# A fifth of the score products, and two residual sums, made on GpSimd in a four-layer graph network

## The chip, the cores and the metric

One NeuronCore of a Trainium2 chip runs the whole kernel. The metric is device time in microseconds. Every run in this study was in the fast state, so all comparisons are of like with like. Engine names are those of the profile: PE (matmuls), PEld (weight loads), DVE (VectorE), ACT (ScalarE), POOL (GpSimd), SP (issues DMAs).

## The reference, cut to what matters

16 graphs of 1024 nodes with 128 features go through four graph layers. The costly one is layer 2, done twice per graph: each edge gets a score from a small network, the scores weigh the adjacency, and messages are summed.

```python
# layer 2, for each of two rounds l (B = 16, N = 1024, D = 128); adjacency has some 1.6% nonzeros
a = x @ We1[l, :D];  b = x @ We1[l, D:]
h = relu(a[:, :, None, :] + b[:, None, :, :] + be1[l])
scores = sigmoid(h @ We2[l] + be2[l])
messages = (adjacency * scores) @ x
... # update by a two-layer network, residual, layer norm
# around every layer: x = x + layer(relu(layernorm(x)))
```

## The kernel before, where the change touches it

The kernel computes scores only for existing edges. Edges of a 128x128 block sit in slots (320, or 480 on the diagonal). One-hot matrices `on`, `om` (fp8), and their transposes `onT`, `omT`, gather node terms to slots and scatter scores back, all by matmuls. A round has nine groups of four blocks: seven off-diagonal (two directions d, so eight products) and two diagonal (four products).

Per group: PE makes `pre`; ACT and DVE make `hid` from it; PE makes `sc`; ACT makes the scores; then this runs:

```python
def scores(self):
    ...
    pt = path.bank("sc", f"pt_{name}")            # scores, slots now on partitions (PSUM)
    ...                                           # u: the scores as two f16 halves (SBUF)
    for d in range(self.nd):
        for i in range(Q):                        # Q = 4
            if i % 2 == 0:
                pair = ...path.m.scratch(...)      # one buffer holds two products
            j = i * self.nd + d
            right = (self.s.omT if d else self.s.onT)[self.grp[i]]
            v = u[:, :, j % J, j // J : j // J + 1]
            nc.vector.tensor_tensor(              # val: the product of one-hot and score
                pair[:, i % 2, :ck], right[:, :ck], v.to_broadcast([P, ck, P]), op=OP.mult
            )
            self.val[d, i] = pair[:, i % 2]

def scatter(self, part):                          # PE; part 0..3, spread over the next group
    ...
    nc.tensor.matmul(self.ps[d][:, i], left[:, k], halves[:, k, :, h], ...)   # reads val
```

Both inputs of a product lie in SBUF: the one-hots and the scores. The residual sums are `nc.vector.tensor_add(xt, xt, o)` at the end of layer 1, and `nc.vector.tensor_add(xt, xt, new)` after layer 2. Each is followed by a layer norm whose statistics DVE makes and whose -0.5 power POOL makes (the only work of POOL).

A scheduler orders every engine's instructions at build time. In the trace of the kernel before, DVE and POOL run theirs in the order built (13 of DVE's 10,759 records could not be matched), so an instruction that waits holds up those behind it.

## Time and profile before

| | before |
|---|---|
| time, median (lowest to highest of 3 runs) | 5532.22 us (5529.48 to 5535.28) |
| PE busy, idle of the span | 5037.3 us, 489.3 us |
| DVE busy | 4304.6 us |
| products on DVE, 128x384 | 1792, 0.55 us each alone, 0.47 us in a row |
| products on DVE, 128x512 (diagonal) | 256, 0.68 us each |
| POOL busy | 184.9 us |

In the lists of groups a line reads: source line, engine, operation, output<-inputs, shape, count, then busy us, mean ns of one, idle time of the engine before it, and what ended that. "Burst" below means the eight products of an off-diagonal group, from the start of the first to the end of the last: median 3.84 us. There are 224 such bursts (16 graphs, two rounds, seven groups). PE's idle time is its span less its busy time. An edit above a line moves its number: the products stand at L1075 before and L1077 after.

### The profile page before, as it was taken

The page shows a single profiled execution, that of the slowest core. Times are in us where ns is not written, and L with a number is a line of the kernel's source. Part 1 is how long each engine was busy: PE and PEld are TensorE (multiplying, and loading weights), DVE is VectorE, ACT ScalarE, POOL GpSimd, SP SyncE. Part 2 cuts the span into 40 slices and gives each one's busy share as a digit, 9 for nine tenths or more (in the row PEclk, how much of TensorE's full clock was granted, in tenths as well). Part 3 has the DMA queues.
Part 4 walks back from the last instruction along what each step waited for, and adds up shares of the span by engine and source line. Part 5 has one row for each costly group of instructions (what it writes and reads, how often), then busy time and mean ns, then how long its engine had stood idle before and what let it go on. Part 6 is the DMA issues. An engine that isn't in the chain of part 4 may idle for free.

```text
span 5526.6 us, 113576 instructions
## 1 busy us (share of the span) xinstructions
PE 5037.3 (91%) x45109; PEld 3719.3 (67%) x45109; DVE 4304.6 (78%) x10759; ACT 3054.6 (55%) x6790; POOL 184.9 (3%) x137
## 2 busy tenths in 40 slices
PE   5999999999999999999999999999999999999996
PEld 4676766667676666666766666676766767666664
DVE  4777787878879787787877878778787887978886
ACT  4555564655647555465555646556465564655543
POOL 0000000000000000000000000000000000000000
PEclk8999999999999999999999999999999999999998
DMA  6242424243242433424334142432424324243111
GB/s 174 62 136 87 121 68 137 76 125 101 84 140 66 125 96 92 131 66 120 98 102 124 56 139 81 122 106 71 140 72 128 97 85 133 67 124 95 54 63 51
DMA packets 740139, 554.56 MB, mean 100 GB/s; under 512 B 32272, under 2 KB 686352, under 8 KB 739600
## 3 DMA queue, kind: packets, MB, share of 16 engines
q1 hardware_dynamic: 734496, 545.58, 33.6%
q8 instruction: 356, 5.83, 0.4%
q10 hardware_dynamic: 5104, 1.65, 0.1%
q14 instruction: 183, 1.50, 0.1%
HBM read 446.44 MB, written 100.66 MB: 99 GB/s over the span
## 4 chain that ended last, share of the span: by engine, by line
PE 47%; DVE 27%; DMA 9%; ACT 9%; issue 4%; POOL 3%; SPq 0%; ACTq 0%; DVEq 0%; POOLq 0%
PE pre L986 11%; DVE val L1075 10%; PE p L1097 6%; DMA at<-in_adj_dram 4%; DVE hid L1003 4%; PE nb L288 4%; PE msg L1114 4%; PE bb L296 3%; PE sc L1018 3%; DMA a<-adjT 2%; DVE omT L854 2%; PE hp L505 2%; POOL st L243 2%; PE h L342 2%; PE tn L743 2%
## 5 line engine op out<-in xcount | busy, mean ns | idle before, releaser
L1003 DVE SCALAR_TENSOR_TENSOR hid<-pre,hid 128x320 f16<-128x320 f32 (+1 forms) x2048 | 993.0, 504 | 294.9 <-ACT hid L1002 283.9
L1002 ACT ACTIVATE hid<-pre 128x320 f16<-128x320 f32 (+1 forms) x2048 | 900.7, 454 | 501.3 <-PE pre L986 473.4
L986 PEld LDWEIGHTS <-part 128*128 128x128 f16 x8192 | 753.4, 98 | 450.5 <-issue 236.2
L986 PE MATMUL pre<-on,part 128*128 128x320 fp8e4 (+1 forms) x4096 | 966.2, 309 | 71.6 <-DVE hid L1003 60.6
L986 PE MATMUL pre<-om,part 128*128 128x320 fp8e4 (+1 forms) x4096 | 994.3, 309 | 0.0
L1114 PE MATMUL msg<-upd,xf 128*128 128x128 f32 (+3 forms) x3008 | 613.6, 323 | 2.2 <-DVE upd L1105 2.2
L1075 DVE TENSOR_TENSOR val<-onT,u 128x384 f32<-128x384 fp8e4 (+1 forms) x1152 | 607.8, 580 | 4.0
L1097 PE MATMUL p<-val,omT 128*128 128x128 f16 x6528 | 534.2, 219 | 29.8 <-DVE val L1075 27.7
L1097 PEld LDWEIGHTS <-omT 128*128 128x128 fp8e4 x6528 | 436.7, 96 | 84.4 <-DVE val L1075 34.4
L1075 DVE TENSOR_TENSOR val<-omT,u 128x384 f32<-128x384 fp8e4 x896 | 439.2, 549 | 0.0
L861 ACT ACTIVATE om<-pm 128x320 fp8e4<-128x320 f32 (+1 forms) x576 | 268.9, 467 | 294.4 <-PE pm L817 285.8
L1114 PEld LDWEIGHTS msg<-upd,xf 128*128 128x128 f32 x3008 | 414.2, 191 | 25.6 <-DVE upd L1105 13.9
L1105 DVE SCALAR_TENSOR_TENSOR upd<-p,adj 128x512 f32<-128x512 f32 x512 | 348.5, 681 | 82.4 <-PE p L1097 82.2
L1097 PE MATMUL p<-val,onT 128*128 128x128 f16 x4480 | 374.1, 219 | 1.4 <-DVE upd L1105 1.4
L847 ACT ACTIVATE onT<-pn 128x384 fp8e4<-128x384 f32 (+1 forms) x576 | 297.6, 517 | 102.7 <-PE pn L817 82.8
L1039 ACT ACTIVATE srow<-sc,be_s,down 128x128 f32<-128x128 f32 (+2 forms) x512 | 259.7, 540 | 168.2 <-PE sc L1018 166.9
L505 PE MATMUL hp<-wh,e 128*128 128x129 f32 x2048 | 318.3, 285 | 22.3 <-DVE e L502 22.3
L1097 PEld LDWEIGHTS <-onT 128*128 128x128 fp8e4 x4480 | 304.6, 97 | 36.9 <-issue 8.8
L505 PEld LDWEIGHTS hp<-wh,e 128*128 128x128 f32 x2048 | 275.5, 195 | 51.9 <-DVE e L502 29.6
L804 ACT ACTIVATE far<-iota_off,mid 128x384 f16<-128x384 f16 x448 | 269.5, 625 | 39.9 <-DVE on L808 34.3
L288 PE MATMUL nb<-z,ct 128*128 128x128 f32 x2048 | 279.3, 282 | 12.4 <-DMA ct<-in_adj_dram 11.9
L1018 PE MATMUL sc<-hid,slide 128*32 128x320 f16 (+1 forms) x4096 | 268.3, 315 | 18.2 <-DVE hid L1003 15.7
(220 smaller groups left out, 8106.8 us busy)
## 6 DMA issues: line engine op xcount, KB each, us to landing
at<-in_adj_dram SPq DMA_DIRECT2D x128, 512.0 KB, 4.3
ct<-in_adj_dram SPq DMA_DIRECT2D x128, 512.0 KB, 4.6
adjT<-tn SPq DMA_DIRECT2D x128, 512.0 KB, 5.1
l<-adjT SPq DMA_DIRECT2D x128, 512.0 KB, 4.2
adj<-adjT SPq DMA_DIRECT2D x256, 256.0 KB, 3.4
a<-adjT SPq DMA_DIRECT2D x128, 384.0 KB, 3.5
adj<-adjT SPq DMA_DIRECT2D x448, 64.0 KB, 2.1
adj<-adjT SPq DMA_DIRECT2D x192, 128.0 KB, 2.6
```

What stands on the lines that cost most here:

```text
L288: nc.tensor.matmul(ps, mat[:, k], z[:, k], start=(k == 0), stop=(k == T - 1))
L505: nc.tensor.matmul(sums[:, t], e[:, i, t * P : (t + 1) * P], wh[:, k + i, : D + 1], start=False, stop=True, skip_group_check=True,)
L804: nc.scalar.activation(far[:, : ck * P], self.iota[t == u][:, : ck * P], AF.Abs, bias=s.mid[:, i : i + 1])
L847: nc.scalar.activation(onT, pn[:, : ck * P], AF.Copy, saturate=False)
L986: nc.tensor.matmul(pre[:, :c], path.parts[node // Q][:, k, node % Q, v], hot[:, :c], start=(hot is on and k == 0), stop=(hot is om and k = ...
L1002: nc.scalar.activation(hid[:, 0, :c], pre[:, :c], AF.Relu)
L1003: nc.vector.scalar_tensor_tensor(hid[:, 1, :c], pre[:, :c], 0.0, hid[:, 0, :c], op0=OP.max, op1=OP.subtract)
L1018: ins = nc.tensor.matmul(self.sc[g * G : (g + 1) * G, : self.c], self.path.slide[:, self.l, G - 1 - r : 2 * G - 1 - r], self.hid[self.done ...
L1075: nc.vector.tensor_tensor(pair[:, i % 2, :ck], right[:, :ck], v.to_broadcast([P, ck, P]), op=OP.mult)
L1097: nc.tensor.matmul(self.ps[d][:, i], left[:, k], halves[:, k, :, h], start=(k, h) == terms[0], stop=(k, h) == terms[-1],)
L1105: nc.vector.scalar_tensor_tensor(upd, self.ps[d], S_SCALE, self.adj[:, d * Q : (d + 1) * Q], op0=OP.add, op1=OP.mult,)
L1114: nc.tensor.matmul(self.msg[h][:, (lo - h * Q) * P : (hi - h * Q) * P], self.xf[mb // Q][:, mb % Q], up, start=False, stop=True, skip_grou ...
```

## The change

The intent: DVE is busy 78% and POOL 3%, so POOL should take some of DVE's work. Two of the eight products of an off-diagonal group (d = 1, i = 2 and 3: those that scatter reads last) and both sums move.

```diff
-            nc.vector.tensor_add(xt, xt, o)
+            nc.gpsimd.tensor_tensor(xt, xt, o, op=OP.add)
@@ scores
-                        nc.vector.tensor_tensor(
+                        engine = nc.gpsimd if d and i >= Q // 2 else nc.vector
+                        engine.tensor_tensor(
                             pair[:, i % 2, :ck], right[:, :ck], v.to_broadcast([P, ck, P]), op=OP.mult
                         )
@@ last
-            nc.vector.tensor_add(xt, xt, new)
+            nc.gpsimd.tensor_tensor(xt, xt, new, op=OP.add)
```

## The prediction

> **What bounds the kernel now.** I read, in order: busy shares and slices of the page, waits of PE, DVE's groups by form, the chain that ended last, and DVE's and POOL's timelines around single instructions.
>
> Busy shares, and the slices in tenths:
>
> ```profile
> PE 5037.3 (91%) x45109; PEld 3719.3 (67%) x45109; DVE 4304.6 (78%) x10759; ACT 3054.6 (55%) x6790; POOL 184.9 (3%) x137
> ...
> PE   5999999999999999999999999999999999999996
> ...
> DVE  4777787878879787787877878778787887978886
> ```
>
> PE is busy nine tenths of every slice but the first and last, whether DVE has 7 or 9 tenths in that slice: 127.6 us of 138 where DVE has 127.6 (1656 to 1794 us), 128.5 where DVE has 98.3 (1518 to 1656). So PE sets the time and DVE's load hardly moves its pace. PE was idle 5526.6 - 5037.3 = 489 us, and only that can be won. The table of waits says who ended PE's idle times (us in total, times, longest):
>
> ```profile
> PE pm L817 <- DVE omT L854: 65.6, 70, 1.9
> PE tp L260 <- ACT h L252: 63.1, 31, 12.7
> PE pre L986 <- DVE hid L1003: 60.6, 101, 2.1
> PE p L1097 <- DVE val L1075: 27.7, 58, 1.2
> ```
>
> Adding the rows whose releaser is DVE gives some 250 us: omT 68, hid 80, val 28, e 22, xf 17, own 15, the rest small. The other half is ACT, DMA, start and end. PE hardly waits for val itself; it waits for omT and hid, which may stand behind a burst of val in DVE's in-order queue. The chain of waits says the same: PE 47%, DVE 27%, of which val is 10%:
>
> ```profile
> PE 47%; DVE 27%; DMA 9%; ACT 9%; issue 4%; POOL 3%; SPq 0%; ACTq 0%; DVEq 0%; POOLq 0%
> ```
>
> **The skill, and this trace.** The Trainium skill's "GPSIMD Engine Reference", section "Performance versus the Vector engine", gives 2.6 cycles of 1.2 GHz per element for a two-input elementwise instruction, 4497 ns for 2048 floats. POOL ran none of that kind here, only the power for the layer norms, so no row confirms it. "SBUF — State Buffer", section "Who interferes with whom", says that a DVE instruction with two SBUF inputs and a POOL instruction that reads SBUF exclude each other for a whole instruction. One direction is in this trace. Timeline of POOL and then DVE, first where DVE ran nothing of the kind, then where it was inside L500 (two SBUF inputs); start, length, both in us:
>
> ```profile
> 2641.97 1.01 POOL L243 TENSOR_TENSOR st_y<-st_y,half_neg 128x4 f32<-128x4 f32 x1 [30.81 <-DVE st_y L242]
> ```
> ```profile
> 2676.20 1.65 POOL L243 TENSOR_TENSOR st_y<-st_y,half_neg 128x4 f32<-128x4 f32 x1 [5.34 <-DVE st_y L242]
> ...
> 2676.03 0.94 DVE L500 SCALAR_TENSOR_TENSOR e<-e 128x768 f32<-128x768 f32 x1
> ```
>
> L500 ends at 2676.97 and the power 0.88 later. Behind a val product (274.57 to 275.26) a power took 1.38 and ended 0.86 after it. So POOL is held until DVE's instruction is over. The other direction isn't tested: the power reads four or eight elements and lets go; the 47 two-input DVE instructions that overlapped a power ran at most 3% over their median. "Perfetto Trace Analysis", section "Optimizing Scalar/DVE Operations", warns that moving work between these two might not help.
>
> **The change, part by part.**
> Products. Of nine groups a round, seven are off-diagonal with eight products each; the two of d = 1, i = 2 and 3 go to POOL. 16 batches x 2 rounds x 7 x 2 = 448 of 2048 products, a bit over a fifth. Groups by form, and four in a row in the timeline:
>
> ```profile
> L1075 DVE TENSOR_TENSOR val<-omT,u 128x384 f32<-128x384 fp8e4 x896 | 439.2, 549 | 0.0
> ```
> ```profile
> 2600.85 1.95 DVE L1075 TENSOR_TENSOR val<-onT,u 128x384 f32<-128x384 fp8e4 x4
> 2602.71 1.96 DVE L1075 TENSOR_TENSOR val<-omT,u 128x384 f32<-128x384 fp8e4 x4
> ```
>
> In a row each costs DVE (1.95 - 0.55) / 3 = 0.47 us, since ends overlap. DVE loses 448 x 0.47 = 210 us, 0.94 per group. On POOL one is estimated from the skill's figures at 384 x 2.6 / 1.2 = 0.83 plus some 0.1 of start, 0.93 us; 448 make 417 us.
> Residual sums. 32 of 128x1024, 1.22 us each on DVE, 39 us in all; on POOL 2.3 us each by the same estimate (half of 4497 ns), 74 us. POOL would go from 185 to some 675 us, 12%, plus holds. It has the room.
> So on paper DVE loses 250 us and goes to 4055 us, 73%. Little of that lies on PE's path. I looked at each idle time of PE that DVE ended and at the unbroken run of DVE work before the releasing instruction: runs with products in them precede 147 us of these; with every product in them a quarter cheaper, at most 95 us go. Removed waits come back partly as later ones, as the uniform PE row says; I take 40%, a choice: 40 us, or 0.7%.
>
> What is added. A POOL product is needed late: scatter takes d = 1, i = 2 and 3 last, and in the group at 2600 us the d = 1 matmuls run from 2611.9 to 2613.7, over 10 us after the scores at 2600.6. Two products of 0.93 fit, even held. But the power now shares POOL's in-order queue with them: 128 powers, perhaps one in six finding a product ahead. And each residual sum has a layer norm behind it, so that chain grows by 1.1 us plus a hold, 32 times. PE waited for this very chain in the row tp <- h above. Estimate: 32 x 1.5 + 20 = 70 us of added latency, a third of it reaching PE: 20 us lost.
>
> The scheduler also lays everything out anew: by the built order, some 27,000 of 69,000 rows of PE stand otherwise than before, and a third of DVE's. I give that plus or minus 25 us with no sign.
>
> **The rivals.**
> A, DVE keeps the port. Products come back to back on DVE; if POOL gets the port only when the burst is over, DVE has its whole 0.94 us a group, POOL's two run beside hid, upd and omT, which read one tile from PSUM. Time: 5532 - 40 + 20 = about 5510 us.
> B, the port alternates. POOL's two products become ready at the same moment as DVE's six. If POOL, once waiting, takes the port when the current DVE product ends, the next DVE product waits the 0.85 us that POOL reads. DVE then gives 2 x 0.85 for a gain of 0.94 and ends 0.76 us later per group: 170 us more DVE work, with some 50 of stalls behind POOL's sums. DVE would show about 4450 us. The mirrored sensitivity costs PE 35 us, with the 20 of latency 5532 + 55 = 5587, less where DVE has slack: 5555 us. For B speaks the skill's "whole instruction" and that the layout makes both start together; against it, that no DVE instruction was slowed by a power.
> C, a product waits in POOL's queue behind a power whose input comes late, PE meets its scatter too early and stalls; or a power waits behind a product whose scores come late. POOL is over 80% idle and the slack is 10 us, so I hold it rare, but each case costs several us: up to 100 us, 5600 to 5650.
> D, nothing reaches PE's path: 5530 plus or minus 15.
>
> **Range and chances.** Weights: A 0.35, B 0.35, C 0.1, D 0.2, which gives 0.35 x 5510 + 0.35 x 5555 + 0.1 x 5620 + 0.2 x 5530 = 5541. As the sums and products moved look like chosen shares, not all or half, somebody may have found this share good; I shade down to 5525 us. Range 5450 to 5610. Faster by over 2% needs 5422, that is 110 us out of the 250 that PE waits for DVE at all: 0.06. Slower by over 2% needs 5643, C or a bad B: 0.10. Within 2%: 0.84.
>
> **What would show it.** In the profile after: DVE's busy time near 4055 (A) or above 4300 (B). The mean of remaining products on DVE stays at 550 ns (A) or grows to some 700 or more (B); POOL's products near 0.9 us, or longer by holds. PE's idle time by who ended it: rows of omT and hid smaller in A; rows of val with POOL as releaser and tp <- h larger in C. PE's busy time should stay at 5037 within 15 us.
> I am wrong if PE's idle time falls by over 100 us (then the bursts were worth more than my count of runs), if a POOL product takes two or more us (then POOL's queue becomes the wait), or if the new order alone moves PE by more than 1%.

## The result, and the profile after

The changed kernel is correct and takes 5603.97 us (median of 4 runs, 5592.23 to 5611.10), against 5533.75 us for the kernel before in the same rounds. The ratio is 1.0125, 95% interval 1.0104 to 1.0146. A ratio here is the mean time of one kernel's fast runs over that of the other's in the same rounds, so it is not quite the ratio of the medians.

The busy shares and the slices of the changed kernel:

```profile
PE 5066.5 (90%) x45109; PEld 3750.6 (67%) x45109; DVE 4332.1 (77%) x10279; ACT 3074.2 (55%) x6790; POOL 729.9 (13%) x617
...
PE   5989999999999999899999999999999998999886
...
DVE  4777787877879777797877878778797777978786
```

DVE ran 480 instructions fewer (10,759 to 10,279) and yet was busy 27 us longer. POOL gained 545 us. PE's idle time grew by 51 us (489.3 to 540.5) and its busy time by 29 us for the same 45,109 matmuls. These two make the longer span. The clock granted to PE was lower as well: PE spent 302 us at half rate against 142 (more on this below).

DVE's and POOL's groups by form show where DVE's time came from:

```profile
L1077 DVE TENSOR_TENSOR val<-onT,u 128x384 f32<-128x384 fp8e4 x896 | 685.7, 822 | 2.6
L1077 DVE TENSOR_TENSOR val<-omT,u 128x384 f32<-128x384 fp8e4 x448 | 227.9, 544 | 0.0
```
```profile
L1077 POOL TENSOR_TENSOR val<-omT,u 128x384 f32<-128x384 fp8e4 x448 | 469.3, 1067 | 2734.7 <-DVE u L1063 1876.4 <-ACT hid L1002 399.4 <-ACT e L501 322.2
L334 POOL TENSOR_TENSOR x<-x,o 128x1024 f32<-128x1024 f32 x16 | 40.1, 2507 | 358.5 <-DVE o L333 334.3 <-ACT rank L841 24.2
L1204 POOL TENSOR_TENSOR xb<-xb,y 128x1024 f32<-128x1024 f32 x16 | 37.6, 2352 | 57.1 <-DVE y L369 57.1
```

The same products in the kernel before:

```profile
L1075 DVE TENSOR_TENSOR val<-onT,u 128x384 f32<-128x384 fp8e4 x896 | 443.2, 551 | 3.0
```

The products with `onT`, the first four of a burst, take 822 ns in the mean where they took 551. Those with `omT`, the last of it, take 544 ns, as before (549). One burst in the timelines of POOL and of DVE (start, length, in us):

```profile
1579.77 1.93 POOL L1077 TENSOR_TENSOR val<-omT,u 128x384 f32<-128x384 fp8e4 x2 [2.50 <-issue]
```
```profile
1579.88 3.18 DVE L1077 TENSOR_TENSOR val<-onT,u 128x384 f32<-128x384 fp8e4 x4
1582.98 1.01 DVE L1077 TENSOR_TENSOR val<-omT,u 128x384 f32<-128x384 fp8e4 x2
```

While POOL makes its two products (1579.77 to 1581.70), DVE's first four take 3.18 us in place of 1.95. POOL done, the next two take 1.01 us for two, as they should. Taken one by one, 418 of DVE's 1344 products of this size last over 600 ns, 1134 ns in the mean, about one for each of POOL's 448. The burst of six takes 4.17 us (median); the burst of eight took 3.84. POOL's own products take 829 ns at best and 1139 in the median, so POOL is held too: the engines take turns.

PE feels it first at the products it wants first:

```profile
PE p L1099 <- DVE val L1077: 134.6, 270, 1.1
PE pre L986 <- DVE hid L1003: 106.6, 81, 3.0
PE tp L260 <- ACT h L252: 51.3, 33, 13.8
PE pm L817 <- DVE omT L854: 4.5, 10, 1.0
```

PE's waits for val rose from 28 to 135 us and those for hid's buffers from 61 to 107; the waits for omT fell from 66 to 5. The releaser of val is DVE in these rows, not POOL. The view of the chain that ended last broke off after 2% of this span, so it is not used.

### The profile page after: what moved, and what is told of

It is laid out like the page before. It is cut to its first block, busy times and chain, and to the rows that moved or that the text cites. A ratio compares the mean times of both kernels' runs of the same rounds, so it can differ in the third digit from the quotient of the medians.

```text
span 5607.0 us, 114252 instructions
## 1 busy us (share of the span) xinstructions
PE 5066.5 (90%) x45109; PEld 3750.6 (67%) x45109; DVE 4332.1 (77%) x10279; ACT 3074.2 (55%) x6790; POOL 729.9 (13%) x617
## 5 line engine op out<-in xcount | busy, mean ns | idle before, releaser
L986 PE MATMUL pre<-on,part 128*128 128x320 fp8e4 (+1 forms) x4096 | 985.5, 310 | 115.0 <-DVE hid L1003 106.6
L1077 DVE TENSOR_TENSOR val<-onT,u 128x384 f32<-128x384 fp8e4 (+1 forms) x1152 | 849.2, 791 | 3.7
L1077 POOL TENSOR_TENSOR val<-omT,u 128x384 f32<-128x384 fp8e4 x448 | 469.3, 1067 | 2734.7 <-DVE u L1063 1876.4
L1099 PE MATMUL p<-val,omT 128*128 128x128 f16 x6528 | 572.0, 219 | 142.3 <-DVE val L1077 134.6
L1099 PEld LDWEIGHTS <-omT 128*128 128x128 fp8e4 x6528 | 448.1, 97 | 232.9 <-issue 169.2
L854 DVE TENSOR_TENSOR omT<-pq,odd_off 128x384 fp8e4<-128x384 f32 x448 | 247.1, 552 | 47.1 <-PE pq L850 42.1
```

The lines of the kernel that those rows point to most:

```text
L986: nc.tensor.matmul(pre[:, :c], path.parts[node // Q][:, k, node % Q, v], hot[:, :c], start=(hot is on and k == 0), stop=(hot is om and k = ...
L1077: engine.tensor_tensor(pair[:, i % 2, :ck], right[:, :ck], v.to_broadcast([P, ck, P]), op=OP.mult)
```

## The experiments

All twelve ran correctly, but for one that is wrong on purpose. "Theory of the port" in the expectations is rival B of the prediction: POOL and DVE keep each other out while one reads. They ran in three calls of four (e1 to e4, e5 to e8, e9 to e12); those of one call shared a chip and the runs of the kernel before. Two facts about order come from comparing the built programs, instruction by instruction, without buffer numbers (counted as the lines of a text diff):

| pair | PE instructions that stand otherwise, of 74,643 |
|---|---|
| before, changed kernel | 14,597 |
| before, e4_spare; before, e9_spare_third; e11_late_ctl, e12_late_spare | 0 (also 0 on DVE and ACT) |
| e1_products, e5_gone | 148 |
| before, e8_copies | 11,226 |
| e3_late, e10_late_one | some 12,800 |

The pairs with no or hardly any difference measure one effect by itself. In the others the scheduler's new order is part of the result.

### The two halves of the change: e1_products and e2_sums

e1 undoes the two sums, e2 undoes the products:

```diff
 # e1_products: the changed kernel, but
-            nc.gpsimd.tensor_tensor(xt, xt, o, op=OP.add)      (and the same for `new`)
+            nc.vector.tensor_add(xt, xt, o)
 # e2_sums: the kernel before, but
-            nc.vector.tensor_add(xt, xt, o)                    (and the same for `new`)
+            nc.gpsimd.tensor_tensor(xt, xt, o, op=OP.add)
```

> The 448 products on POOL as in the change, both residual sums back on DVE. Theory of the port (a POOL product holds back the DVE product beside it for its reading): the DVE products with onT of 384 columns still take some 820 ns in the mean, against 551 before, PE still waits over 100 us for val, and the time is 5570 to 5595 us, most of the loss. Theory of the sums (the loss is the wait of DVE's layer norm statistics for POOL's sum, and the power behind it in POOL's queue): 5525 to 5540 us. Theory of the new order: anything from 5530 to 5600, without a relation to the products' durations.

Measured: 5577.76 us against 5528.04, ratio 1.0091 (1.0074 to 1.0108). Products with `onT` took 835 ns, PE waited 143.5 us for val. As the theory of the port had it: most of the loss is the products'.

> Only the two residual sums on POOL, all products on DVE. Theory of the port: products at 551 ns in the mean, some DVE instructions with two SBUF inputs held up to 2 us behind a sum, about 32 us of DVE waiting for the sum before the statistics; 5540 to 5565 us. Theory of the sums: 5590 to 5610 us, the whole loss.

Measured: 5537.71 us, ratio 1.0017 (1.0008 to 1.0026), below the band expected. Thirteen of DVE's products were held behind a sum and lasted 2.6 us in the mean, but DVE waited only 12 us for sums in front of statistics: the order had put other work there. In the changed kernel's order it waited 39 us. One of those, in the timelines of POOL, DVE and PE of the changed kernel:

```profile
1339.05 2.53 POOL L334 TENSOR_TENSOR x<-x,o 128x1024 f32<-128x1024 f32 x1 [23.80 <-DVE o L333]
```
```profile
1341.61 0.49 DVE L232 BATCH_NORM_STATS2 bn<-x 128x6 f32<-128x128 f32 x2 [2.24 <-POOL x L334]
```
```profile
1347.55 0.46 PE L986 MATMUL pre<-on,part 128*128 128x320 fp8e4 x2 [2.13 <-DVE hid L1003]
```

The statistics stand next in DVE's queue and wait 2.24 us; `hid` stands behind them, late, and PE stops for 2.13 us. The sums on top of e1 cost 26 us in the changed kernel, 10 alone. How much of the 26 is these waits, how much the other order and how much the clock (214 us at half rate in e1, 302 in the changed kernel) was not separated.

### The hold by itself: e4_spare and e9_spare_third

Everything stays on DVE, and POOL makes products that nobody reads, into a dead constant tile:

```diff
                         self.val[d, i] = pair[:, i % 2]
+                        if d and i >= Q // 2:
+                            spare = we2_rows.rearrange("p l d -> p (l d)").bitcast(F16)
+                            nc.gpsimd.tensor_tensor(
+                                spare[:, : ck * P].rearrange("p (c n) -> p c n", n=P),
+                                right[:, :ck], v.to_broadcast([P, ck, P]), op=OP.mult
+                            )
 # e9_spare_third: one block of 128 columns (spare[:, :P], right[:, :1], v[:, :1]) in place of three
```

> The kernel before with all products and sums on DVE, and on POOL the 448 products a second time, into a tile nobody reads (half-width output). Nothing waits for POOL here. Theory of the port: DVE's onT products again take 750 to 850 ns, DVE's busy time rises from 4305 to 4500 to 4600 us, and the time to 5600 to 5680 us. Theory of POOL's lateness or its queue: 5525 to 5540 us, as nothing reads the results and only the 128 powers share the queue.

Measured: 5750.67 us, ratio 1.0411 (1.0394 to 1.0429). DVE's busy time rose by 253 us to 4557.7, and 446 of its products were held. Its groups by form:

```profile
L1075 DVE TENSOR_TENSOR val<-onT,u 128x384 f32<-128x384 fp8e4 x896 | 696.6, 830 | 3.0
L1075 DVE TENSOR_TENSOR val<-omT,u 128x384 f32<-128x384 fp8e4 x896 | 438.2, 545 | 0.0
```

PE, DVE and ACT stand in exactly the order of the kernel before and nothing waits for POOL's results, so this is the hold alone: 222 us of time (5750.67 - 5528.04) for 253 us of DVE, 0.88 us for each. The burst went from 3.84 to 5.11 us, 0.63 us for each POOL product. DVE's busy time met the expectation; the time, 5750.67, lies above the band I had given.

> As e4_spare (PE, DVE and ACT stand in exactly the order of the kernel before), but POOL's spare products cover one block of 128 columns, not three. If a DVE product is held for as long as POOL reads, some 0.28 us in place of 0.83, the hold of 0.58 us falls to 0 to 0.1 us a product, DVE's busy time rises by under 50 us and the time is 5530 to 5570 us. If a hold costs the same whatever POOL's size (a fixed handing over of the port), the time stays near 5650 to 5750.

Measured: 5574.70 us against 5531.93, ratio 1.0078 (1.0062 to 1.0095). The time is just above the band. POOL's product now took 398 ns alone; the median burst rose by 0.36 us, 0.18 for each. DVE's busy time rose by 59 us, a little over what was expected, the time by 43 us. Its groups:

```profile
L1075 DVE TENSOR_TENSOR val<-onT,u 128x384 f32<-128x384 fp8e4 x896 | 477.5, 586 | 3.0
L1081 POOL TENSOR_TENSOR we_rows<-omT,u 128x128 f16<-128x128 fp8e4 x448 | 231.6, 517 | 2914.5 <-DVE u L1057 2896.9
```

Only 194 products were held here (731 ns in the mean), as 250 of POOL's 448 shorter products were over before the burst began; part of the hold fell on other DVE work (the copy at L1063 took 229 ns against 171). In the 67 groups with two held products the burst rose by 0.36 us over the same group of the kernel before, and by 1.27 us in the 222 such groups of e4. So, where it strikes, the hold follows POOL's length: 0.63 us for 0.83 us, 0.18 us for 0.40 us, in both cases POOL's length less some 0.2 us. A cost that is the same whatever POOL's length is excluded.

### The products away from the burst: e3_late, and its control pair e11_late_ctl and e12_late_spare

POOL reads the scores from a copy that DVE makes after its own last product. The first copy only ties the second to that product:

```diff
-                        engine = nc.gpsimd if d and i >= Q // 2 else nc.vector
+                        engine = nc.vector
+                        if d and i >= Q // 2:
+                            engine = nc.gpsimd
+                            late = we2_rows.rearrange("p l d -> p (l d)")[:, : 2 * CK_OFF]
+                            late = late.rearrange("p (c i) -> p c i", i=2)
+                            if i == Q // 2:
+                                nc.vector.tensor_copy(late, self.val[1, 1][:, :ck, :2])
+                                nc.vector.tensor_copy(late, u[:, :, 1::2, 1])
+                            v = late[:, :, i - Q // 2 : i - Q // 2 + 1]
```

> As e1_products, but POOL's two products of a group read their scores from a small copy that DVE makes after its own last product of the group, so that POOL starts when DVE's burst is over (two small DVE copies a group, some 0.2 us, are added). Theory of the port: DVE's products go back to about 551 ns, PE's waits for val fall under 50 us, the time is 5495 to 5535 us. If POOL's products are simply too slow or too late for PE, they are now later still, and the time stays at that of e1_products or rises.

Measured: 5381.48 us, ratio 0.9738 (0.9722 to 0.9754), faster than both kernels and below the band I had given. No product on DVE was held. Groups by form of DVE and POOL, and PE's waits for val:

```profile
L1085 DVE TENSOR_TENSOR val<-onT,u 128x384 f32<-128x384 fp8e4 x896 | 438.6, 551 | 2.5
L808 DVE TENSOR_SCALAR on<-far,wid 128x384 fp8e4<-128x384 f16 x448 | 211.4, 484 | 21.8 <-ACT far L804 18.4 <-PE pre L986 1.6
```
```profile
L1085 POOL TENSOR_TENSOR val<-omT,we_rows 128x384 f32<-128x384 fp8e4 x448 | 382.8, 875 | 3160.2 <-DVE we_rows L1083 2456.2 <-PE p L1107 349.5 <-PE pn L817 93.4
```
```profile
PE p L1107 <- DVE val L1085: 7.7, 18, 0.8
```

DVE's `onT` products are back at 551 ns, POOL's near its 829. Some of the hold moved to L808, a one-input instruction from f16 in SBUF, up from 413 to 484 ns. PE's waits for val fell to 8 us although POOL's products are now made later than in the change: they were hardly ever late for PE (its waits for them come to 1.8 us).

The sums are on DVE here, and PE's order differs from both kernels, so the control pair repeats the contrast with e4 under equal order. Both make all eight products on DVE and then the two copies; e12 adds POOL's spare products reading the copy:

```diff
                         self.val[d, i] = pair[:, i % 2]
+                        if d and i == Q - 1:
+                            ...   # late, as above
+                            nc.vector.tensor_copy(late, self.val[1, 3][:, :ck, :2])
+                            nc.vector.tensor_copy(late, u[:, :, 1::2, 1])
 # e12_late_spare only:
+                            for n in range(2):
+                                nc.gpsimd.tensor_tensor(spare..., self.s.omT[self.grp[2 + n]],
+                                    late[:, :, n : n + 1].to_broadcast([P, ck, P]), op=OP.mult)
```

> Control for e12: the kernel before with the two small DVE copies after all eight products, POOL without products. DVE has 448 x 0.08 = 36 us more: 5540 to 5570 us by the slope of e4_spare (0.88 us for 1 us of DVE), give or take what the order does.

Measured: 5503.48 us, ratio 0.9937 (0.9919 to 0.9954): faster than the kernel before although DVE was busy 31 us longer. The expectation failed; besides the copies only the order differs (see below).

> As e11_late_ctl, in exactly its order on PE, DVE and ACT, with POOL's 448 spare products of 384 columns, which read the copy and so start when DVE's burst of eight is over. Theory of the port: DVE's products keep their 551 ns, and only what DVE runs next with two SBUF inputs[...] is held; 10 to 60 us over e11_late_ctl, where the same products beside the burst cost 222 us in e4_spare. If POOL's work costs wherever it stands, about 200 us.

Measured: 5520.04 us, ratio 0.9978 (0.9970 to 0.9987), 16.6 us over e11. Every product on DVE kept its 0.55 us:

```profile
L1075 DVE TENSOR_TENSOR val<-onT,u 128x384 f32<-128x384 fp8e4 x896 | 441.9, 550 | 2.6
L1075 DVE TENSOR_TENSOR val<-omT,u 128x384 f32<-128x384 fp8e4 x896 | 440.1, 549 | 0.0
L500 DVE SCALAR_TENSOR_TENSOR e<-e 128x512 f32<-128x512 f32 x64 | 56.1, 877 | 0.0
```

The hold did not vanish but fell on other work: L500 with 512 columns took 680 ns in e11, and DVE was busy 51 us longer than there (4386.2 against 4335.2). The same POOL work in the same number costs 222 us beside the burst and 17 us behind it.

### What the relief is worth: e5_gone

Here nobody makes the 448 products; scatter reads the ones of i - 2 instead. The result is wrong on purpose.

```diff
+                        if d and i >= Q // 2:
+                            self.val[d, i] = self.val[d, i - 2]
+                            continue
```

> Wrong result on purpose: the 448 products are made by nobody, and scatter reads those of i - 2 in their place; sums on DVE. This is what taking them off DVE is worth with no POOL at all. If time follows DVE's burst (so far 0.66 to 0.99 us a group for changes of -0.94 to +1.27 us of burst, some 0.7 of it), the burst falls from 3.84 to 2.82 us and the time to 5350 to 5390 us. If the gain of e3_late came from its new order and not from DVE's relief, this has another order and may lie anywhere from 5400 to 5540. By the prediction's sensitivity (40 us for 210 us of DVE) it would be 5490.

Measured: 5361.09 us against 5525.83, ratio 0.9706 (0.9690 to 0.9722), DVE busy 4103.8 us. This meets the band of the burst theory. Its order is all but that of e1_products, so the two are subtracted (they ran in different calls, where the kernel before differed by 2 us): making those products on POOL beside DVE's costs 5577.76 - 5361.09 = 217 us, with 259 us more on DVE (4363.1 - 4103.8). That agrees with e4's 222 for 253. Against the kernel before, taking the products away is worth 165 us for 201 us of DVE, 0.82 us for each, a new order included.

### The control for order: e8_copies, and the variants e10_late_one, e6_late_half, e7_late_sums

e8 is e3 with `engine = nc.vector` throughout: POOL makes no product.

> Control of e3_late: the same code and the same two small DVE copies a group, but the two late products are made by DVE too; POOL does no product. Theory of the burst: the burst is some 0.2 us longer than before, so 5535 to 5570 us. If it was the new order or the copies that gained, 5380 to 5450.

Measured: 5471.65 us, ratio 0.9903 (0.9887 to 0.9920). This missed its band. DVE was busy 17 us longer than before, and the time fell by 54 us. Nothing but the order and two tiny copies a group differs. The burst grew, to 5.37 us (median), as the order put other DVE work between its products. That the copies themselves gained the 54 us is not excluded by a run, but they add work. So the order moves this kernel by an amount near what the change lost, and of e3's 147 us against the kernel before, a part is the order's; 90 us is its gain over e8, which shares its source but not its order.

e10 merges e3's two copies into one instruction:

```diff
-                                nc.vector.tensor_copy(late, self.val[1, 1][:, :ck, :2])
-                                nc.vector.tensor_copy(late, u[:, :, 1::2, 1])
+                                nc.vector.scalar_tensor_tensor(
+                                    late, self.val[1, 1][:, :ck, :2], 0.0, u[:, :, 1::2, 1],
+                                    op0=OP.mult, op1=OP.add)
```

> As e3_late, with one small DVE instruction a group in place of two (it reads both the last product and the scores). It saves 224 x 0.08 = 18 us of DVE, some 15 us of time: 5360 to 5375 us, if the new order does not count. The orders of PE differ in 12,800 of 74,600 instructions, and orders moved the time by up to 70 us so far, so 5310 to 5450 is possible.

Measured: 5455.08 us, ratio 0.9853 (0.9837 to 0.9870). DVE was busy 22 us less than in e3 (4173.6 against 4195.8) and the time is 74 us longer, above even the wide band. This is the same lottery from the other side.

e6 sends all four products of d = 1 to POOL, in e3's manner (`if d:` for `if d and i >= Q // 2:`, the copy made at i = 0).

> As e3_late, but all four products of d = 1 of an off-diagonal group go to POOL, 896 in all, after DVE's burst of four. DVE's burst falls to 2.0 us. Theory of the burst: 0.7 x 1.84 us x 224 groups less than before, 5230 to 5290 us, if POOL's four products (3.4 us and holds) are there when PE wants them. If POOL's time counts: PE waits for POOL's val for over 50 us and the time is 5330 to 5450 us.

Measured: 5408.41 us, ratio 0.9792 (0.9776 to 0.9809): inside the band of the theory that POOL's time counts, 27 us slower than e3. DVE was busy 4082.9 us, 113 less than in e3. But PE waited only 3.3 us for POOL's products, where that theory asked for over 50, so its mechanism fails, and the burst theory fails by its band. L808 rose to 496 ns and the mean of a 128x128 `has` product from 285 to 368, so DVE's other work was held more. What took the rest of the expected gain is open; order is one candidate.

e7 is e3 with both sums on POOL.

> As e3_late with both residual sums on POOL as in the change. The sums alone cost 0.17% in e2_sums; if they cost the same here, 5385 to 5400 us against 5381. If the sums and products disturb each other in POOL's queue (the change lost 20 to 25 us more than e1_products), 5400 to 5420.

Measured: 5453.97 us, ratio 0.9868 (0.9851 to 0.9884), 72 us over e3 and above both bands. DVE waited only 6 us for sums. PE's orders of e3 and e7 differ in 12,058 instructions, which by e8 and e10 may be enough for that; the sums' own share was not separated.

## Why the prediction was right, and where it was not

The time, 5604 us, fell inside the range, and within 2%, but near the upper edge, 79 us above the point that was given and 49 above rival B's own figure. It got there by two errors that partly cancel, so the hit is in part luck.

- **Which rival.** B happened: the port alternates. The prediction gave it 0.35 and saw the reason, that both engines start together. A is excluded by the 418 held products, D by the loss of 70 us. B is shown by the held products in the change, by e4 under equal order, and by e12, where the hold of products vanishes when POOL starts later. That it is the shared SBUF port is what the Trainium skill ("SBUF — State Buffer", "Who interferes with whom") gives as explanation; the runs show the exclusion, not the wire.
- **The size of the hold.** The step "the next DVE product waits the 0.85 us that POOL reads" was too large: 0.63 us of burst for each POOL product. So DVE ended 0.33 us later per group (3.84 to 4.17), not 0.76, and was busy 4332 us, not "about 4450".
- **What DVE's time is worth.** This step failed: "at most 95 us go", of which 40% was taken, "40 us, or 0.7%" for 210 us of DVE, or 0.19 us for each. Measured: 0.88 (e4) and 0.72 (e9: 43 us for 59) under the order before, 0.84 between e1 and e5, 0.82 for the relief in e5. The worth depends on where the work stands: behind the burst (e12 less e11) 51 us of DVE cost 17, or 0.33. The reading behind the prediction's figure, that DVE's load "hardly moves" PE's pace as PE is at nine tenths in every slice, was wrong. (Its 127.6 us of PE from 1656 to 1794 us is 127.4 in the view, which changes nothing.) In e4, PE's row still shows nothing but eights and nines in the middle while PE lost 150 us more to idling; its busy time rose by 72 us as well, in e5 it fell by 38. So PE's busy time was not a fixed floor, as "should stay at 5037 within 15 us" had it, and the count of direct waits for DVE missed most of the path. Why the same matmuls take more or less of PE's busy time is settled in part only.
- **The granted clock.** One part is the clock, which the prediction left out. In the kernel before, the 128x128 matmuls of `p` start 58 ns apart at full rate and 107 at half. So half of PE's busy time within the spells at half rate is an estimate of what the low clock adds: 48 us before, 93 in e4, 109 in the changed kernel, 58 in e5. With equal order in e4, this part, 45 of the 72 us, follows from the hold. In the changed kernel the estimate grew by 61 us, more than PE's whole busy time did, and in e5 by some 10 while the busy time fell, so the rest is not settled.
- **The net of the products.** With the measured terms, in shares of the time before: taking the products off DVE -2.94% (e5), making them on POOL in nearly that order +3.85% (e5 to e1), the sums with their order +0.34%: together +1.25%, the result. The prediction's A, 5510 us, was as far off as B: with the hold away and both sums on POOL the kernel takes 5454 us (e7); with the sums on DVE 5381 in one order and 5455 in another.
- **POOL's length.** 0.93 us was estimated, 0.83 measured for a product; 2.3 us against 2.35 to 2.5 for a sum. Both were good enough.
- **Latency of the norms and C.** The 20 us for sums and powers compare with 10 (e2) and 26 (on top of e1). PE's row tp <- h did not grow (63 to 51 us; all its tp L260 rows together went from 84 to 88), and no row names POOL as the releaser of val. C did not happen.
- **The new order.** "Plus or minus 25" was too small. e8 and e10 show 54 and 74 us, in either direction (e8: 54 us faster with 17 us more on DVE; e10: 74 us slower than e3 with 22 us less). So the prediction's own sign of being wrong, an order that moves the time by more than 1%, came true between e3 and e10. By the estimate above the low clock took 31 us in e3 and 65 in e10 and in e7 each, so nearly half of those two distances goes with it.

## What to carry to other kernels

Before moving an elementwise product to POOL, ask what DVE runs at that same moment: beside DVE instructions with two SBUF inputs the work cost more than it saved, and the same POOL work placed a few microseconds later was nearly free. Price an engine's relief by an experiment, taking the work away with a wrong result or adding spare work that leaves the order as it was, and not by the busy row of the engine that looks saturated. Such a price holds for the place where the work stands (0.88 beside the burst, 0.33 behind it). Where a scheduler lays out the program, compare orders before believing a 1% difference, and keep one control with equal order.

## What the Trainium skill lacked or had wrong

- "SBUF — State Buffer", "Who interferes with whom", has the exclusion, and it holds in both directions here. It says that issue order decides who blocks, but not what happens in a stream: POOL got in between two DVE products that otherwise follow each other without a gap, about one held DVE product for each POOL product (418 held, 448 made).
- The same page, in "SBUF: two separate sides", has the loser blocked for the whole instruction. Measured by the lengths in the profile it is less: DVE's burst lost 0.63 us for a POOL product of 0.83 us, 0.18 us for one of 0.40 us. POOL's lengths without their fixed 0.18 us (next point) are 0.65 and 0.22 us, close to what DVE lost, so the exclusion may cover only the part that grows with the columns; two sizes don't prove that.
- "GPSIMD Engine Reference", "Performance versus the Vector engine", gives 2.6 cycles per element for two inputs. The sums of two floats agree (2.34 us at best for 1024 columns, 2.7 cycles each with all overhead). The products, fp8 times a repeated float, are cheaper: from 398 ns for 128 columns and 829 ns for 384, a column costs 1.68 ns, 2.0 cycles of the page's 1.2 GHz, and 0.18 us is fixed.
- "TensorE: Matmul & The Clock Gate", "HAM oscillation — how this bites in real kernels", warns of idle gaps over 3.4 us. In the clock records of the kernel before, a single gap of 1.63 us (ending at 1088 us; under 2.0 us of idle in the 14 us before) already came ahead of 3.4 us at half rate. Of the 15 gaps of 1.6 to 1.7 us that ended at full rate, five were followed by half rate within 6.8 us. The gaps are by the profile's modelled ends of matmuls.
